# Gathers two steps ahead, each in two halves, and the maxima's three parts summed on VectorE

## The chip, the cores and the metric

The kernel runs on one core of a Trainium2 chip. A core has five engines with queues of their own: TensorE (PE; its weight loads are shown apart, as PEld), VectorE (DVE), ScalarE (ACT), GpSimd (POOL) and SyncE (SP). Each engine works through its own instructions strictly in order, and waits on semaphores for what others make. SP only issues plain DMAs here, and POOL issues the indirect ones (gathers by a list of row numbers). SBUF is the working memory, with 128 partitions; PSUM is what TensorE writes to.

The metric is the device time of one execution in microseconds. Times before: a median of 1243.95 us over 14 runs, from 1241.13 to 1253.4.

## The reference

One layer of attention on a graph of 3125 nodes with 128 features and 100000 edges, of five types. The edges are sorted by destination. For each type r:

```python
q = x[dst] @ W_Q[r]; k = x[src] @ W_K[r]; v = x[src] @ W_V[r]     # 8 heads of 16
logits = (q * k).sum(-1) / 4 + attn_bias[r]
max_v = segment_max(logits, dst)                 # per node, type and head
exp_l = exp(logits - max_v[dst])
attn = exp_l / (segment_sum(exp_l, dst)[dst] + 1e-12)
out += segment_sum(attn * v, dst)
```

Only the edges of type r take part in round r. After that come a projection, a residual and a layer norm, and once more a residual and a layer norm. The result has 3125 x 128 values.

## The kernel before, in words

**Tables.** A first part, up to about 100 us, computes for every pair of node and type the rows of k and v (`kv_d`, 256 values a row), stores them in HBM, and prepares for each edge the number of its row (`idx`). q is computed block by block in the main loop, and stored as three bf16 parts.

**Groups.** The 100000 edges are cut into 196 groups of 512 (`GE`), so that a group is four tiles of 128 edges (`T` = 4). For each group POOL issues four indirect DMAs (`gather`, line 681), one for each tile, each fetching 128 rows of 1 KB into a kv buffer. There are `KVB` = 22 kv buffers, used in turn, each with a pool of its own. Nine of them (`KVA`) lie outside the memory of the first part.

**Steps.** The main loop has steps k from -2 to some 220. Step k does the logits of group k: VectorE multiplies kv with the q of each edge (`prod`, L759), sums over each head (`lg`, L760), and SP stores the result to HBM (L765). The q of each edge comes from TensorE (`qe`, L746), which multiplies a 0/1 matrix `hot` (from `spot`, L737) with the q of the nodes of the group's window. Step k also weighs group v = k - 19, for v from 22 on (16 to 18 behind for the first groups), whose maxima are known by then: `weigh` (L881) multiplies the v half of the kv buffer with the exponentials. It is the last reader of that kv buffer.

**Maxima.** The nodes come in 25 blocks of 128, about eight groups each. One step after the last group that may hold an edge of the block, `maxima_load` issues on POOL one indirect DMA that gathers the stored logits of the block (`ell`, L772, 2304 bytes for each of 128 nodes). In the three steps after that VectorE makes the maxima (`mine` L795, `wl` L810, `mx` L816; before the first of them ScalarE copies `ell` to `by_head`, L787). They are split into three bf16 parts (`m3`), stored, and fetched for each group as `mw` on SP's queue. The block's first group is weighed eight steps after its last logits.

**Spreading the maxima.** One step before a group is weighed, `spread_m` brings the maxima of the nodes to the edges with TensorE: for each of four tiles, and each of the three parts, one matmul (L863) of `hot` with `mw`, the three parts being accumulated in PSUM. Its output is repeated `times` = 8 times (12 where there are no logits to do any more); only the first copy is read. `less_max` (L872, VectorE) subtracts it from the logits, in place in PSUM, `exps` (L876, ScalarE) takes the exponential, and `weigh` and `weights` (L889) read that. `sums` (L915, L917, L924) then sums the weighed rows of each node with TensorE.

**The order.** The order of the instructions on each engine is that in which the loop writes them out. Waits are derived from the buffers: an instruction that writes a buffer waits for the last reader of what was there. In step k the loop writes first SP's fetches, then the gathers of all groups up to k + 2 (`AHEAD` = 2; k + 1 in the last sixteen steps before the last group), then the ell gather if one is due; `spread_m` of the next group, `sums`, `spread_q`; and on VectorE `weigh`, `less_max` (for the next step), `norm` (L936 to L939), `logits`, `spot`, and the step's share of q's remainders (L717, L726), maxima and norms. A step is thus some 2.9 us of VectorE's time in the lightest case, and more with maxima or norms in it.

**Blocks as the prediction uses them.** A block of the loop is taken to be the time from one ell gather's start to the next one's, eight steps apart as a rule.

Of the kernel before, what the change touches and what calls it, by code (L numbers as in the profile page):

```python
# [8 lines left out]
F32 = mybir.dt.float32  # L9
BF16 = mybir.dt.bfloat16  # L10
I32 = mybir.dt.int32
AF = mybir.ActivationFunctionType
ALU = mybir.AluOpType
AX = mybir.AxisListType
# [3 lines left out]
P = 128  # L18
# [4 lines left out]
HEADS = 8  # L23
# [17 lines left out]
T = GE // P  # L41
NGR = -(-E // GE)
# [4 lines left out]
WR = WN * R  # L47
# [6 lines left out]
AHEAD = 2  # L54
# [5 lines left out]
SB = P * E // N // SR  # L60
SPAD = 5
QB = 3
KVB = 22
HELD = 21
KVA = 9


@with_exitstack
# [40 lines left out]
def full_at(n, more=0):  # L109

    last = E // N * n + slack(n) + more
    return -(-min(E, last) // GE) - 1 if n < N else NGR - 1
# [17 lines left out]
NM = len(MB)  # L130


def windowed_path(
# [4 lines left out]
    nc = tc.nc  # L138
# [4 lines left out]
    kv_d = dram.tile([((NT - 1) * P + 64) * R, KVW], F32, name="kv_d")  # L143
# [6 lines left out]
    def keep(name, shape, dt=F32):  # L150
        return const.tile(shape, dt, name=name)

    idx = keep("idx", [P, T, NGR], I32)
# [19 lines left out]
    def buffers(those):  # L173
        for i in those:
            kvs_[i] = ctx.enter_context(tc.tile_pool(name=f"kvp{i}", bufs=1)).tile(
                [P, T, KVW], F32, name=f"kv{i}"
            )

    at_once = range(KVA)
    buffers(at_once)  # L180
# [171 lines left out]
    live = {}  # L352
# [290 lines left out]
    rows, counted = {}, 0  # L643
# [29 lines left out]
    ps = ctx.enter_context(tc.tile_pool(name="ps", bufs=2, space=PSUM))  # L673
    buffers(i for i in range(KVB) if i not in at_once)
    hold = ctx.enter_context(tc.tile_pool(name="hold", bufs=HELD))
    flow = ctx.enter_context(tc.tile_pool(name="flow", bufs=2))
    late_flow = ctx.enter_context(tc.tile_pool(name="late_flow", bufs=2))
    def gather(g):
        kv = kvs_[g % KVB]
        for t in range(T):  # L680
            nc.gpsimd.indirect_dma_start(  # L681
                out=kv[:, t, :], out_offset=None, in_=kv_d[:, :],
                in_offset=bass.IndirectOffsetOnAxis(ap=idx[:, t, g : g + 1], axis=0),
            )


    def fetch_x(name, b):
# [68 lines left out]
    def logits(g):  # L756
        kv, lg = kvs_[g % KVB], live["lg", g]
        prod = flow.tile([P, T, H], F32, name="prod", bufs=1)
        nc.vector.tensor_tensor(prod, kv[:, :, :H], live.pop(("qe", g)), op=ALU.mult)  # L759
        nc.vector.tensor_reduce(  # L760
            lg[:, :, :HEADS], prod.rearrange("p t (k d) -> p t k d", d=HD), AX.X, ALU.add
        )

    def store_logits(g):
        nc.sync.dma_start(  # L765
            lg_d[g * GE : (g + 1) * GE, :].rearrange("(p t) c -> p (t c)", t=T),
            live["lg", g].rearrange("p t c -> p (t c)"),
        )

    def maxima_load(b):  # L770
        ell = late_flow.tile([P, D, LW], F32, name="ell", bufs=1)
        nc.gpsimd.indirect_dma_start(  # L772
            out=ell.rearrange("p s c -> p (s c)"), out_offset=None,
            in_=lg_d[: (full_at(MEND[b], D) + 1) * GE, :],
            in_offset=bass.IndirectOffsetOnAxis(ap=start_i[:, b : b + 1], axis=0),
        )
        live["ell", b] = ell
# [78 lines left out]

    def spread_m(g, times):

        me = ps.tile([P, T, times, 2, HEADS // 2], F32, name="me", tag="me")
        hot, mw = live.pop(("hot", g)), live.pop(("mw", g))  # L860
        for t in range(T):
            for s in range(3):
                nc.tensor.matmul(  # L863
                    me[:, t], hot[:, t, :],
                    mw[:WR, None, :, s, :].to_broadcast([WR, times, 2, HEADS // 2]),
                    start=(s == 0), stop=(s == 2),
                )
        live["mde", g] = me[:, :, 0].rearrange("p t h k -> p t (h k)")

    def less_max(g):  # L870
        mde = live["mde", g]
        nc.vector.tensor_tensor(mde, live.pop(("lg", g))[:, :, :HEADS], mde, op=ALU.subtract)  # L872

# [4 lines left out]
    def weigh(g):  # L878
        wv, kv = late_flow.tile([P, T, PW], F32, name="wv"), kvs_[g % KVB]
        live["wv", g] = wv  # L880
        nc.vector.tensor_tensor(  # L881
            wv[:, :, :H].rearrange("p t (k d) -> p t k d", d=HD),
            kv[:, :, H:].rearrange("p t (k d) -> p t k d", d=HD),
            live["mde", g][:, :, :, None].to_broadcast([P, T, HEADS, HD]),
            op=ALU.mult,
        )
# [131 lines left out]
    step_of, n = {}, 0  # L1018
# [3 lines left out]
    group_at = {k: g for g, k in step_of.items()}  # L1022
    final = step_of[NGR - 1]
# [5 lines left out]
    full_step = [step_of[full_at(n, D)] for n in MEND]  # L1029
# [3 lines left out]
    at_k, k = {}, 0  # L1033
    for v in range(NGR):
        k = max(k + 1, ready[block_of(v, MEND)])
        at_k[v] = k
    v_at = {k: v for v, k in at_k.items()}
# [19 lines left out]

    gathered = 0
    for gathered in range(KVA):
        gather(gathered)  # L1060
    assert all(q_from[b] >= 2 for b in range(QB, NT))
    for k in range(-2, root_at[NT] + 2):
        v, g = v_at.get(k), group_at.get(k)
        q_step = {k - f: b for b, f in enumerate(q_from) if b >= QB and -2 <= k - f <= 5}

        if k >= 0 and k + 3 in group_at:
            fetch_keys(group_at[k + 3])
            fetch_q(group_at[k + 3])
        if -2 in q_step:
            fetch_x("xq", q_step[-2])  # L1070
        for b in range(NT):
            if done_at[b] - 1 == k:
                fetch_x("xr", b)
            if norm_at[b + 1] + 1 == k:
                store_z(b)
        for b in range(NM):
            if ready[b] - 3 == k:
                store_m(b)
        if 5 in q_step:
            store_q(q_step[5])  # L1080
        for u in range(NGR):
            if max(at_k[u] - 3, ready[block_of(u, MEND)] - 2) == k:
                fetch_m(u)

        while gathered < NGR - 1 and step_of[gathered + 1] <= k + (AHEAD if k < final - 16 else 1):
            gathered += 1
            gather(gathered)
        for b in range(NM):
            if full_step[b] + 1 == k:
                maxima_load(b)  # L1090

        for b in range(NT):
            if done_at[b] + 1 == k:
                residual(b)
        if v_at.get(k - 4) is not None:
            by_node(v_at[k - 4])
        if v_at.get(k - 2) is not None:
            carry(v_at[k - 2])
        if 1 in q_step:
            turned(q_step[1])  # L1100
        if 3 in q_step or 4 in q_step:
            second_part()
        if 2 in q_step or 3 in q_step:
            first_part()

        if v_at.get(k + 1) is not None:
            spread_m(v_at[k + 1], 8 if k + 1 in group_at else 12)
        if v_at.get(k - 1) is not None or v_at.get(k - 3) is not None:
            sums(v_at.get(k - 1), v_at.get(k - 3))
        if k + 1 in group_at:  # L1110
            spread_q(group_at[k + 1])

        if v is not None:
            weigh(v)
        if v_at.get(k + 1) is not None:
            less_max(v_at[k + 1])
            exps(v_at[k + 1])
        if v is not None:
            weights(v)
        if k + 1 in group_at:  # L1120
            types(group_at[k + 1])
        if v_at.get(k - 2) is not None:
            norm(v_at[k - 2])
        if g is not None:
            logits(g)
            store_logits(g)
        if k + 2 in group_at:
            spot(group_at[k + 2])
        if v_at.get(k + 1) is not None:
            places(v_at[k + 1], 2 if k >= final - 1 else 0)  # L1130
        if 3 in q_step or 4 in q_step:
            third_part()
        if 2 in q_step or 3 in q_step:
            remainder()
        for b in range(NM):
            whole = MB[b][2] is None
            if ready[b] - 6 == k and whole:
                maxima(b, 0, 2)
            if ready[b] - 5 == k and whole:
                maxima(b, 2, 4)  # L1140
            if ready[b] - 4 == k:
                maxima(b, 4 if whole else 0, R)
        for b in range(NT):
            if done_at[b] == k:
                project(b)
        for b in range(NT + 1):
            if root_at[b] == k:
                roots(b)
            if norm_at[b] == k:
                norms(b)  # L1150
        if 0 in q_step:
            turn_q(q_step[0])
        if 1 in q_step:
            queries(q_step[1], 0, RH)
        if 2 in q_step:
            queries(q_step[2], RH, R)
# [505 lines left out]
```

## Time and profile before

| | |
|---|---|
| median of 14 runs | 1243.95 us |
| the profiled execution, whole | 1242.57 us |
| its span, first to last instruction | 1240.8 us |
| busy: PE, DVE, ACT, POOL | 858.4, 931.2, 633.4, 799.5 us |
| granted TensorE clock, mean | 0.793 |
| gathers of kv | 784, from 89.8 to 1161.2 us |
| ell gathers | 25, from 150.1 to 1169.2 us |
| mean busy time of one gather | 0.95 us |

The page gives for each engine the busy time, its share of the span and the number of instructions. A line of a group of instructions gives the source line, the engine, the operation, the tiles (out<-in), the count, the busy time in us and the mean of one in ns, and after the second bar the idle time of the engine just before them with its main releaser. A line of the waits gives the waiting instruction, what ended the wait, the total in us, the number of waits and the longest. A line of the timeline gives start and duration in us, engine, line, operation and tiles, and in brackets the idle time of the engine before it. The name of a releaser is inferred: it is the last event seen before the wait ended, and not always the cause.

### The profile page before, as it was taken

Reading aid. Unit: us, or ns where it says so; the run is one execution under the profiler, and the core shown is the slowest. Engines: PE = TensorE matmul, PEld = TensorE weight load, DVE = VectorE, ACT = ScalarE, POOL = GpSimd, SP = SyncE. Lnnn points to the kernel's source line nnn. Section 1 sums busy time; section 2 is a strip of 40 time slices with the busy share of each in tenths; the row PEclk is TensorE's granted clock in tenths of the full one; section 3 lists DMA queues with packets and bytes.
Section 4 is the critical chain, followed back from the end, with each engine's and each line's share of the span. In section 5 each row is a group of like instructions: output and inputs, shape, how many; then the busy total and the mean of one; then the engine's idle time right before and its main releaser. Section 6 shows DMA issues by size and latency. Waiting matters only on the chain.

```text
span 1240.8 us, 25686 instructions
## 1 busy us (share of the span) xinstructions
PE 858.4 (69%) x7526; PEld 675.3 (54%) x7526; DVE 931.2 (75%) x2559; ACT 633.4 (51%) x2248; POOL 799.5 (64%) x901
## 2 busy tenths in 40 slices
PE   7984356667676777687777677767767767776784
PEld 3543244456555555566565555555656555565573
DVE  4554376688787778878877887877977878789886
ACT  2560033454564565566456456555645645646463
POOL 1627777776777767676766776766767677767300
PEclk9995556787877878778678788778877878879797
DMA  6997666766676676666676667666666666666300
GB/s 165 322 326 201 169 157 171 184 161 146 180 167 159 170 172 151 168 182 166 155 162 169 159 168 175 149 164 172 163 149 175 161 156 178 169 151 158 93 8 18
DMA packets 180889, 203.63 MB, mean 164 GB/s; under 512 B 83207, under 2 KB 146083, under 8 KB 180620
## 3 DMA queue, kind: packets, MB, share of 16 engines
q0 software_dynamic: 40896, 113.39, 33.2%
q1 hardware_dynamic: 135414, 83.80, 28.9%
q10 hardware_dynamic: 4430, 4.71, 1.5%
q8 instruction: 63, 1.03, 0.3%
q14 instruction: 86, 0.70, 0.2%
HBM read 166.50 MB, written 35.28 MB: 163 GB/s over the span
## 4 chain that ended last, share of the span: by engine, by line
DMA 24%; DVE 24%; PE 21%; issue 12%; POOL 11%; ACT 5%; SPq 2%; DVEq 0%; ACTq 0%; POOLq 0%
POOL kv L681 11%; DMA kv<-kv_d,idx 8%; DMA ell<-lg_d,start_i 6%; PE pp L915 6%; DMA mw<-m_d 4%; DVE wl L810 4%; PE pr L395 4%; DVE prod L759 3%; PE me L863 3%; DVE wv L881 3%; PE qe L746 2%; DVE mx L816 2%; DVE lg L760 2%; PE pp L917 2%; DVE hot L737 2%
## 5 line engine op out<-in xcount | busy, mean ns | idle before, releaser
L681 POOL DMA_INDIRECT kv<-kv_d,idx x784 | 744.8, 950 | 268.1 <-issue 195.9
L915 PE MATMUL pp<-wv,at 128*125 128x136 f32 x1568 | 351.9, 358 | 1.6 <-DVE o L939 1.6
L915 PEld LDWEIGHTS pp<-wv,at 128*125 128x125 f32 x1568 | 264.7, 234 | 62.5 <-issue 60.1
L863 PE MATMUL me<-mw,hot 125*128 125x64 bf16 (+1 forms) x2352 | 127.2, 211 | 162.6 <-DMA mw<-m_d 90.6
L901 ACT ACTIVATE at<-row_at,nkey 128x125 f32<-128x125 f32 x744 | 237.5, 398 | 0.0
L746 PE MATMUL qe<-qw,hot 125*128 125x128 bf16 x2352 | 202.3, 248 | 40.0 <-DVE hot L737 36.6
L863 PEld LDWEIGHTS <-hot 125*128 125x128 bf16 x2352 | 114.1, 110 | 194.3 <-issue 97.4
L876 ACT ACTIVATE me<-me 128x32 f32<-128x32 f32 x196 | 35.7, 182 | 358.9 <-DVE me L872 358.3
L746 PEld LDWEIGHTS <-hot 125*128 125x128 bf16 x2352 | 188.1, 121 | 46.0 <-DVE hot L737 44.1
L759 DVE TENSOR_TENSOR prod<-kv,qe 128x512 f32<-128x512 f32 x196 | 133.0, 678 | 34.7 <-DMA kv<-kv_d,idx 31.5
L760 DVE TENSOR_REDUCE lg<-prod 128x32 f32<-128x512 f32 x196 | 134.5, 686 | 6.8
L881 DVE TENSOR_TENSOR wv<-kv,me 128x512 f32<-128x512 f32 x196 | 132.5, 676 | 4.3 <-PE pp L915 4.2
L917 PE MATMUL pp<-pt,carried 125*5 125x136 f32 x390 | 92.0, 325 | 55.1 <-ACT pt L930 54.2
L904 ACT ACTIVATE at<-at 128x500 f32<-128x500 f32 (+1 forms) x196 | 117.3, 599 | 6.2
L707 PE MATMUL prq<-wq,xTq 128*128 128x384 f32 (+1 forms) x88 | 53.6, 705 | 85.2 <-DVE rem L717 85.2
L872 DVE TENSOR_TENSOR me<-lg,me 128x32 f32<-128x32 f32 x196 | 37.5, 191 | 94.5 <-PE me L863 90.0
L810 DVE TENSOR_TENSOR wl<-by_head,shut 128x1024 f32<-128x1024 f32 (+2 forms) x73 | 76.9, 1053 | 13.7 <-ACT by_head L787 11.0
L816 DVE TENSOR_REDUCE mx<-wl 128x16 f32<-128x1024 f32 (+2 forms) x73 | 76.5, 1048 | 2.5
L924 PEld LDWEIGHTS pp<-rsum,o 125*128 125x128 f32 x392 | 75.9, 236 | 4.2 <-issue 4.1
L737 DVE TENSOR_SCALAR hot<-kt,row_of 125x512 bf16<-125x512 bf16 x196 | 70.9, 362 | 1.5 <-DMA kt<-key_d 1.1
L924 PE MATMUL pp<-rsum,o 125*128 125x25 f32 x392 | 68.8, 258 | 4.0 <-DVE o L939 4.0
L917 PEld LDWEIGHTS pp<-pt,carried 125*5 125x5 f32 x390 | 18.2, 86 | 93.5 <-ACT pt L930 69.9
(184 smaller groups left out, 981.1 us busy)
## 6 DMA issues: line engine op xcount, KB each, us to landing
kt<-key_d SPq DMA_DIRECT2D x196, 128.0 KB
qw<-q_d SPq DMA_DIRECT2D x196, 96.0 KB
kv_d<-kvs SPq DMA_DIRECT2D x24, 640.0 KB
kv<-kv_d,idx POOLq DMA_INDIRECT x784
q_d<-q SPq DMA_DIRECT2D x22, 480.0 KB
lg_d<-lg SPq DMA_DIRECT2D x196, 18.0 KB
mw<-m_d SPq DMA_DIRECT2D x196, 6.0 KB
xr<-in_x SPq DMA_DIRECT2D x24, 64.0 KB
```

What stands on the lines that cost most here:

```text
L681: nc.gpsimd.indirect_dma_start(out=kv[:, t, :], out_offset=None, in_=kv_d[:, :], in_offset=bass.IndirectOffsetOnAxis(ap=idx[:, t, g : g + ...
L746: nc.tensor.matmul(qe[:, t, :], hot[:, t, :], qw[:WR, s, :], start=(s == 0), stop=(s == 2))
L759: nc.vector.tensor_tensor(prod, kv[:, :, :H], live.pop(("qe", g)), op=ALU.mult)
L760: nc.vector.tensor_reduce(lg[:, :, :HEADS], prod.rearrange("p t (k d) -> p t k d", d=HD), AX.X, ALU.add)
L810: nc.vector.tensor_tensor(wl, by_head[:, None].to_broadcast([P, n, nh, D]), shut[:, :n, None, :].to_broadcast([P, n, nh, D]), op=ALU.add,)
L863: nc.tensor.matmul(me[:, t], hot[:, t, :], mw[:WR, None, :, s, :].to_broadcast([WR, times, 2, HEADS // 2]), start=(s == 0), stop=(s == 2),)
L881: nc.vector.tensor_tensor(wv[:, :, :H].rearrange("p t (k d) -> p t k d", d=HD), kv[:, :, H:].rearrange("p t (k d) -> p t k d", d=HD), live ...
L901: nc.scalar.activation(at[:, t, :], row_at[:, :WR], AF.Abs, bias=nkey[:, t, g : g + 1], scale=1.0)
L904: nc.scalar.activation(at[:, on_dve:], at[:, on_dve:], AF.Relu, bias=1.0, scale=-1.0)
L915: nc.tensor.matmul(pp, at[:, t, :], wv[:, t, :], start=(t == 0), stop=(t == T - 1))
L917: nc.tensor.matmul(pp[:R], carried[:WR, g, :], live.pop(("pt", g - 1)), start=False, stop=False,)
L924: nc.tensor.matmul(op, live.pop(("o5", done)), rsum[:WR], start=True, stop=True)
```

## The change

- `gather` takes two of the four tiles of a group at a time. `first_gathers` does t = 0 and 1, with the row numbers out of `idx` as before. `more_gathers` does t = 2 and 3, and takes the row numbers from a small tile `rows`, which VectorE copies from `idx`.
- In step k, the first half for group k + 2 is written out after `weigh`, and the second half, with its copy, after `logits` and its store. The ell gather, if one is due, comes after that. Before, all of this stood ahead of the step's work. The exception for the last steps (k + 1 instead of k + 2) is gone.
- 21 kv buffers instead of 22; six groups instead of nine are gathered ahead of the loop.
- `spread_m` makes one matmul for each tile, four in all, with all three parts side by side, without accumulation, and with five copies (5 x 24 = 120 columns) where it made twelve matmuls with eight copies (64 columns). `less_max` then sums the three parts with a reduction on VectorE into a tile `mde` in SBUF, which takes the place of the one in PSUM. Where twelve copies were made, after the last logits, nothing changes.

```diff
-KVB = 22
+KVB = 21
-KVA = 9
+KVA = 6
...
-    def gather(g):
+    def gather(g, t0, rows):
         kv = kvs_[g % KVB]
-        for t in range(T):
+        for t in range(T // 2):
             nc.gpsimd.indirect_dma_start(
-                out=kv[:, t, :], out_offset=None, in_=kv_d[:, :],
-                in_offset=bass.IndirectOffsetOnAxis(ap=idx[:, t, g : g + 1], axis=0),
-            )
+                out=kv[:, t0 + t, :], out_offset=None, in_=kv_d[:, :],
+                in_offset=bass.IndirectOffsetOnAxis(ap=rows(t), axis=0),
+            )
+
+    def first_gathers(g):
+        gather(g, 0, lambda t: idx[:, t, g : g + 1])
+
+    def more_gathers(g):
+        rows = flow.tile([P, T // 2], I32, name="rows", bufs=3)
+        nc.vector.tensor_copy(rows, idx[:, T // 2 :, g])
+        gather(g, T // 2, lambda t: rows[:, t : t + 1])
...
     def spread_m(g, times):
+        hot, mw = live.pop(("hot", g)), live.pop(("mw", g))
+        if times < 8:
+            me = ps.tile([P, T, times, 2, 3, HEADS // 2], F32, name="me", tag="me")
+            for t in range(T):
+                nc.tensor.matmul(
+                    me[:, t], hot[:, t, :],
+                    mw[:WR, None].to_broadcast([WR, times, 2, 3, HEADS // 2]),
+                    start=True, stop=True,
+                )
+            live["parts", g] = me[:, :, 0].rearrange("p t h s k -> p t h k s")
+            return
...
     def less_max(g):
+        if ("parts", g) in live:
+            mde = flow.tile([P, T, 2, HEADS // 2], F32, name="mde")
+            nc.vector.tensor_reduce(mde, live.pop(("parts", g)), AX.X, ALU.add)
+            live["mde", g] = mde.rearrange("p t h k -> p t (h k)")
         mde = live["mde", g]
         nc.vector.tensor_tensor(mde, live.pop(("lg", g))[:, :, :HEADS], mde, op=ALU.subtract)
...
     for gathered in range(KVA):
-        gather(gathered)
+        first_gathers(gathered)
+        gather(gathered, T // 2, lambda t: idx[:, T // 2 + t, gathered : gathered + 1])
...
-        while gathered < NGR - 1 and step_of[gathered + 1] <= k + (AHEAD if k < final - 16 else 1):
-            gathered += 1
-            gather(gathered)
-        for b in range(NM):
-            if full_step[b] + 1 == k:
-                maxima_load(b)
...
-            spread_m(v_at[k + 1], 8 if k + 1 in group_at else 12)
+            spread_m(v_at[k + 1], 5 if k + 1 in group_at else 12)
...
         if v is not None:
             weigh(v)
+        ahead_of = []
+        while gathered < NGR - 1 and step_of[gathered + 1] <= k + AHEAD:
+            gathered += 1
+            ahead_of.append(gathered)
+            first_gathers(gathered)
...
         if g is not None:
             logits(g)
             store_logits(g)
+        for u in ahead_of:
+            more_gathers(u)
+        for b in range(NM):
+            if full_step[b] + 1 == k:
+                maxima_load(b)
```

More of the change, by code (lines that the diff above doesn't have):

```diff
@@ L857, in spread_m @@
     def spread_m(g, times):
+        hot, mw = live.pop(("hot", g)), live.pop(("mw", g))
[9 more added lines that the diff above has]
+            return
         me = ps.tile([P, T, times, 2, HEADS // 2], F32, name="me", tag="me")
-        hot, mw = live.pop(("hot", g)), live.pop(("mw", g))
         for t in range(T):
```

## The prediction

> **What bounds the kernel now.** I read the page's totals first, then the waits of POOL and DVE, then the timeline of one block. The totals show that no engine is full; POOL's 64% is an understatement, since an indirect gather is counted with 0.95 us and the next one never starts less than 1.25 us after it.
>
> ```profile
> PE 858.4 (69%) x7526; PEld 675.3 (54%) x7526; DVE 931.2 (75%) x2559; ACT 633.4 (51%) x2248; POOL 799.5 (64%) x901
> ...
> L681 POOL DMA_INDIRECT kv<-kv_d,idx x784 | 744.8, 950 | 268.1 <-issue 195.9
> ```
>
> At 1.25 us, 784 gathers and 25 ell gathers are 1011 us of POOL's time. A group costs POOL 5.0 us, a block of eight groups with its ell gather 33 x 1.25 = 41.25 us. Between the ell gathers at 196.46 and 1078.48 lie 20 blocks, 44.1 us each: POOL has under 3 us to spare per block. DVE's waits:
>
> ```profile
> DVE me L872 <- PE me L863: 90.0, 52, 4.5
> DVE mine L795 <- DMA ell<-lg_d,start_i: 56.9, 21, 6.1
> ...
> DVE prod L759 <- DMA kv<-kv_d,idx: 31.5, 14, 5.2
> ```
>
> kv is hardly waited for, and the timeline shows why: gathers run far ahead. Now the block from the ell gather at 634.89 (step 98; the 196 products of L759, counted, number the steps), first POOL:
>
> ```profile
> 634.89 0.94 POOL L772 DMA_INDIRECT ell<-lg_d,start_i  x1 [3.05 <-ACT lg L753]
> 636.13 0.95 POOL L681 DMA_INDIRECT kv<-kv_d,idx  x1 [0.30 <-DVE hot L737]
> ...
> 657.16 0.94 POOL L681 DMA_INDIRECT kv<-kv_d,idx  x1 [1.18 <-DVE den L936]
> ...
> 668.41 1.15 POOL L681 DMA_INDIRECT kv<-kv_d,idx  x1 [0.30 <-issue]
> ...
> 676.12 0.95 POOL L681 DMA_INDIRECT kv<-kv_d,idx  x1 [0.30 <-issue]
> 679.83 0.94 POOL L772 DMA_INDIRECT ell<-lg_d,start_i  x1 [2.77 <-DMA xq<-in_x]
> ```
>
> Then DVE:
>
> ```profile
> 639.54 0.33 DVE L795 SCALAR_TENSOR_TENSOR mine<-slot,deg,ell 128x64 f32<-128x64 f32 x1 [3.58 <-DMA ell<-lg_d,start_i]
> ...
> 644.52 0.68 DVE L881 TENSOR_TENSOR wv<-kv,me 128x512 f32<-128x512 f32 x1
> ...
> 645.86 0.68 DVE L759 TENSOR_TENSOR prod<-kv,qe 128x512 f32<-128x512 f32 x1
> 646.58 0.69 DVE L760 TENSOR_REDUCE lg<-prod 128x32 f32<-128x512 f32 x1
> ...
> 650.16 0.68 DVE L881 TENSOR_TENSOR wv<-kv,me 128x512 f32<-128x512 f32 x1
> ...
> 656.21 0.68 DVE L881 TENSOR_TENSOR wv<-kv,me 128x512 f32<-128x512 f32 x1
> ...
> 668.33 0.42 DVE L726 TENSOR_TENSOR q<-rem,q 128x256 bf16<-128x256 f32 x1
> ```
>
> The reader is to see three things. (1) POOL issues group 101 at 636.13, though its product is due at 651.49; the last gather of a group is issued 7 to 15 us before its product. (2) At 657.16 POOL starts group 105 just after the weighing of step 102 (656.21 to 656.89): with 22 buffers, the gather of group k+3 is released by the weighing of step k, because weighing runs 19 groups behind. (3) The block is a loop: logits stored, ell gathered, a DVE that stands still for 3.58 us, maxima, weighing, buffers free. POOL had finished at 677.07 and waited 2.77 us for the stored logits.
>
> **The change, part by part.** *One buffer less.* With 21 buffers the weighing of step k releases the gather of k+2, not of k+3: every gather that waits starts one step later. *The second half's release.* t = 2 and 3 wait for a copy that DVE makes after the logits of step k. In step 100 the weighing ends at 645.20 and the logits at 647.27; with the added DVE work the copy is done by about 647.7, while POOL, starting at 645.47, needs two gathers, 2.5 us, to 647.97. So this wait adds nothing where the first half waited; where the first half needn't wait it holds POOL to the same instants (the fill at the start). Behind it on POOL stand the next groups and the ell gather, and for ell ACT's by_head and DVE's mine. The copy itself must wait, on DVE, for gathers of three groups earlier: POOL is never that late, nothing.
>
> *POOL's new order in a block,* with E the start of an ell gather. Group 101 follows at once, to E + 6.25. Group 102 needs the weighing of step 100, which needs ell's maxima: that weighing ended at 645.20, E + 10.31; with 0.27 us from release to start (656.89 to 657.16) group 102 starts at E + 10.6. POOL stands still for 4.3 us that it used to fill with groups 102 and part of 103. Group 103 waits for step 101's weighing, 5.64 us later, group 104 for step 102's, 6.05 us after that; both steps are solid DVE work, so DVE's additions (0.36 us a step, below) count twice. From group 104 on, the weighings of steps 103 to 106 are no later than POOL (3.4, 5.4, 4.8, 2.9 us, plus 0.36 each, against 5.0), though step 105's comes within 0.1 us. Groups 104 to 108 take 5 x 5.0 = 25.0 us, and only then the ell gather, which the change leaves behind group 108. Sum: 10.31 + 0.27 + 5.64 + 0.36 + 6.05 + 0.36 + 25.0 = 48.0 us, where this block took 44.94. The wait of 2.77 us for stored logits is gone, swallowed: the logits of step 105 are stored long before. With the means of the 20 blocks (10.11, 5.66, 5.92) it is 47.7.
>
> *Gathers still in time?* Group 105 would be issued from E + 27.8 to 32.8; the last of its four starts at 31.5 and lands some 3.7 us later (the chain shows 3.68 for one), 35.2; its product is due at about 38.5. Nothing.
>
> *VectorE's additions.* The reduction reads 96 elements: L816 takes 0.69 us for 512 and 1.22 for 1024, 1.04 ns each and 0.16 fixed, so 0.26; less_max depends on it, 0.28 with the gap seen between den and its reciprocal. The copy of two elements a row: between 0.06 (the memset of four) and 0.16 (the reciprocal of two), overlapping its neighbours; 0.08. Together 0.36 us, 0.3 to 0.5, times 196 = 70 us of DVE's time, of which two steps a block lie on the path; elsewhere DVE's stand before ell covers it, and it would cost up to five times 0.36 if that were gone.
>
> *TensorE, ScalarE, SP.* Nothing is moved or added on SP and ScalarE; the exponential, 0.18 us, only reads SBUF instead of PSUM. On PE twelve loads and matmuls of 64 columns become four of 120, 768 columns to 480; me's group takes 0.36 to 0.64 us a step, so at most that is saved, and the wait for its PSUM buffer shrinks. I take nothing: where DVE waits for me, POOL is later still. A gain of 0.3 us there offsets the reduction in step 105. If the shorter matmuls let the clock (0.77 in this block) fall, steps 103 to 105 lengthen; bounds -0.3 and +1 us a block.
>
> *The maxima in SBUF.* The weighing now has both inputs in SBUF. The nearest row is L726, two SBUF inputs: at 668.33 it began 0.08 us before a gather, which took 1.15 us instead of 0.95. Of the gathers that began 0.08 to 0.27 us after an L726 did, those whose start it outlasted by 0.15 us did not grow, and those outlasted by 0.22 to 0.45 us grew by 0.09 to 0.33. A weighing of 0.68 us has some 0.54 us in which a gather can begin so, 0.43 of a 1.25 us cycle, and a mean growth of 0.27: 0.12 us a step, 0.5 us over the steps where POOL is the path. Bounds: 0, and 5 x 0.3 = 1.5 us. I take 0.5: 48.2 us a block. The Trainium skill's page "SBUF — State Buffer", section "Who interferes with whom", speaks against this part: a DVE instruction with two SBUF inputs contends with a GpSimd one that reads SBUF, and the second to issue waits out the first. By that rule taken fully a gather beginning anywhere in a weighing would lose 0.34 us on average with chance 0.54, which I estimate at 0.9 us a block, some 10 us more in all.
>
> *The ends.* Six groups up front instead of nine: POOL reaches the second half of group 6 at 122.3, its copy is ready by 118.4; nothing. After the first ell gather (150.05) the copies hold POOL: the second half of group 13 waits for the product of group 11 (159.47), ready at about 161.2, instead of 153.8 when POOL would come; the ell gather of 196.46 moves by some 2.3 us. The last two long intervals, 1078.48 to 1114.84 (36.4 us, seven groups) and to 1156.23 (41.4), were short because the old condition put ell ahead of one group there; they become about 43.3 and 48.2, 6.9 each. From the last ell on the work is as before.
>
> **Sum.** 20 x (48.2 - 44.1) = 82, + 2.3 + 6.9 + 6.9 = 98 us. The profiled execution took 1242.57 us (span 1240.8): 1340.6. The median of the 14 runs is 1.4 above it: 1342.
>
> **Rivals.** *A, the lead was spare:* gathers lead by 7 to 15 us, 3.7 is needed, a step less is harmless; then only DVE's additions show, between nothing (1244) and 0.36 us in six steps of 22 blocks, 47 us (1291). For it: kv is hardly waited for. Against it: the ell gather shares POOL's queue, and its lateness isn't hidden. *B, faster:* the ell gather no longer waits (57 us in all) and PE is lighter; a POOL that never waits takes 41.25 us a block, 20 x 2.85 = 57 us, 1187. It decides if POOL isn't idle between group 101 and step 100's weighing, that is if that weighing came by E + 6.25 instead of 10.3. Ell alone lands 3.7 to 5.9 us after its issue and by_head adds 1.08: against it. *C, worse:* the ell gather, now right behind others, lands later (5.1 us at 1035.88, where POOL did not wait, against about 4.6), the port costs 1.5, and the steps before 105 come out later than POOL by 0.5: 50.2 us a block, 40 us more, 1382.
>
> **How the numbers follow.** Forecast 0.72, C 0.12, A 0.12 (of it 0.03 with no measurable change), B 0.04. The measurement tells 0.3%, 3.7 us, from no change. Faster 0.04, same 0.03, slower 0.93. The range runs from A's upper end to C, 1290 to 1385; the forecast's own, with the bounds of the unknown costs, is 1315 to 1375.
>
> **What would show it.** Right: ell gathers some 48 us apart, with 1.25 us and no wait before each; POOL idle about 4 us once a block, between its first and second group after ell, released by DVE; DVE's wait for ell longer than 3.6 us. Wrong: ell gathers 44 us apart, DVE busy throughout, or DVE waiting for kv in most steps (then the lead was too short, not the queue).

## The result, and the profile after

The changed kernel takes 1358.07 us (median of 13 runs, 1352.65 to 1360.97) against 1247.23 us for the kernel before (62 runs): 1.0885 times as long, 95% interval 1.0864 to 1.0905. The prediction was 1342 us, with a range of 1290 to 1385.

The profiled execution has a span of 1355.1 us, 114.3 more than before. The totals and POOL's two groups of gathers, from the page:

```profile
PE 880.2 (65%) x6110; PEld 679.3 (50%) x6110; DVE 991.6 (73%) x2926; ACT 645.1 (48%) x2248; POOL 814.9 (60%) x901
...
L681 POOL DMA_INDIRECT kv<-kv_d,idx x404 | 392.2, 971 | 268.7 <-DVE mde L892 154.3
L681 POOL DMA_INDIRECT kv<-kv_d,rows x380 | 367.9, 968 | 136.9 <-issue 72.8
```

The reader is to see that VectorE has got 60 us more work, and that nothing is fuller for it: every engine's share has gone down. What is new is the releaser of the gathers. Before, their idle time was "issue"; now 154 us of it end with L892, the reduction that comes on VectorE just after the weighing (the weighing itself is the cause: L892 is only the last event seen). VectorE's waits on data show the other side:

```profile
DVE mine L804 <- DMA ell<-lg_d,start_i: 122.2, 24, 6.2
DVE prod L768 <- DMA kv<-kv_d,rows: 43.6, 29, 4.5
```

VectorE waited for ell 56.9 us before, and 122.2 now. One block on POOL's timeline, from the ell gather at 685.23:

```profile
685.23 0.95 POOL L781 DMA_INDIRECT ell<-lg_d,start_i  x1 [0.30 <-ACT at L927]
686.48 0.94 POOL L681 DMA_INDIRECT kv<-kv_d,idx  x1 [0.30 <-issue]
...
690.23 0.95 POOL L681 DMA_INDIRECT kv<-kv_d,rows  x1 [0.30 <-issue]
696.65 0.95 POOL L681 DMA_INDIRECT kv<-kv_d,idx  x1 [5.47 <-DVE mde L892]
...
702.64 0.95 POOL L681 DMA_INDIRECT kv<-kv_d,idx  x1 [1.29 <-DVE mde L892]
...
708.91 0.96 POOL L681 DMA_INDIRECT kv<-kv_d,idx  x1 [1.57 <-DVE mde L892]
...
729.27 1.27 POOL L681 DMA_INDIRECT kv<-kv_d,idx  x1 [0.30 <-DMA mw<-m_d]
...
734.60 0.95 POOL L781 DMA_INDIRECT ell<-lg_d,start_i  x1 [0.30 <-ACT at L927]
```

And VectorE in the same block:

```profile
690.71 0.33 DVE L804 SCALAR_TENSOR_TENSOR mine<-slot,deg,ell 128x64 f32<-128x64 f32 x1 [5.53 <-DMA ell<-lg_d,start_i]
...
695.69 0.69 DVE L904 TENSOR_TENSOR wv<-kv,mde 128x512 f32<-128x512 f32 x1
696.30 0.25 DVE L892 TENSOR_REDUCE mde<-me 128x32 f32<-128x96 f32 x1
696.58 0.19 DVE L895 TENSOR_TENSOR mde<-lg,mde 128x32 f32<-128x32 f32 x1
...
698.64 0.20 DVE L692 COPY rows<-idx 128x2 int32<-128x2 int32 x1
698.71 0.35 DVE L746 TENSOR_SCALAR hot<-kt,row_of 125x512 bf16<-125x512 bf16 x1
```

POOL makes one group after ell and then stands still for 5.47 us, until the weighing that needs ell's maxima has ended (695.69 + 0.69 = 696.38; the gather starts 0.27 later). The figures in brackets count the 0.30 us that lies between any two gathers. It is held twice more, by 1.29 and 1.57 us, and after that it works without a pause up to the next ell gather, at 734.60, which waits for nothing but its turn. The block takes 49.4 us. VectorE stands still for 5.53 us at ell, because ell itself comes late.

Worked out from the traces, the means over the 20 blocks between the second and the 22nd ell gather, in us from the start of an ell gather to the first gather of each of the groups after it, and to the next ell:

| kernel | ell landed | group 1 | 2 | 3 | 4 | 5 | 8 | next ell |
|---|---|---|---|---|---|---|---|---|
| before | 4.59 | 1.25 | 6.26 | 11.31 | 16.46 | 22.00 | 37.11 | 44.10 |
| after | 5.00 | 1.25 | 10.19 | 16.47 | 22.73 | 28.10 | 43.85 | 48.95 |
| before, last 16 blocks | 4.58 | 1.25 | 6.26 | 11.32 | 16.51 | 22.18 | 37.31 | 44.31 |
| after, last 16 blocks | 5.03 | 1.25 | 10.96 | 16.96 | 23.26 | 28.41 | 44.03 | 49.15 |

"Landed" is the start of `mine`, which reads it. The last two rows leave out the first four of the 20 blocks: in the first three the weighing runs 16 to 18 groups behind for most of the time, and in all four the first weighing comes sooner after ell. The change costs 4.85 us a block, 97 us over 20 blocks, out of 114.3. Up to the first of these ell gathers there are 2.7 us more (199.20 against 196.46), and the two intervals after the last of them cost 7.2 and 7.9 us (43.54 and 49.25 against 36.36 and 41.39). From the last ell gather but one to the end it is 84.1 us, before 84.5.

### The profile page after: what moved, and what is told of

Its sections match the earlier page's. It is cut to its first block, busy times and chain, and to the rows that moved or that the text cites. A ratio compares the mean times of both kernels' runs of the same rounds, so it can differ in the third digit from the quotient of the medians.

```text
span 1355.1 us, 23244 instructions
## 1 busy us (share of the span) xinstructions
PE 880.2 (65%) x6110; PEld 679.3 (50%) x6110; DVE 991.6 (73%) x2926; ACT 645.1 (48%) x2248; POOL 814.9 (60%) x901
## 4 chain that ended last, share of the span: by engine, by line
DVE 40%; DMA 19%; PE 14%; issue 12%; POOL 6%; ACT 6%; SPq 1%; DVEq 1%; ACTq 0%; POOLq 0%
DMA ell<-lg_d,start_i 8%; POOL kv L681 6%; DVE prod L768 6%; DVE wl L819 6%; DVE wv L904 4%; DMA mw<-m_d 4%; DVE lg L769 4%; DVE mx L825 4%; PE pp L938 4%; DMA kv<-kv_d,rows 3%; PE pr L395 3%; DVE mde L892 2%; ACT by_head L796 2%; DVE den L960 2%; DVE mde L895 2%
## 5 line engine op out<-in xcount | busy, mean ns | idle before, releaser
L681 POOL DMA_INDIRECT kv<-kv_d,idx x404 | 392.2, 971 | 268.7 <-DVE mde L892 154.3
L681 POOL DMA_INDIRECT kv<-kv_d,rows x380 | 367.9, 968 | 136.9 <-issue 72.8
L938 PEld LDWEIGHTS pp<-wv,at 128*125 128x125 f32 x1568 | 276.8, 243 | 132.4 <-issue 66.0
L755 PE MATMUL qe<-qw,hot 125*128 125x128 bf16 x2352 | 222.6, 263 | 44.6 <-DVE hot L746 42.7
L755 PEld LDWEIGHTS <-hot 125*128 125x128 bf16 x2352 | 208.3, 129 | 51.4 <-DVE hot L746 48.9
L899 ACT ACTIVATE mde<-mde 128x32 f32<-128x32 f32 x177 | 40.6, 229 | 365.6 <-DVE mde L895 360.3
L872 PE MATMUL me<-mw,hot 125*128 125x120 bf16 x708 | 87.5, 263 | 71.0 <-DMA mw<-m_d 70.9
L904 DVE TENSOR_TENSOR wv<-kv,mde 128x512 f32<-128x512 f32 x177 | 120.2, 679 | 0.3 <-issue 0.2
L872 PEld LDWEIGHTS <-hot 125*128 125x128 bf16 x708 | 63.2, 123 | 101.9 <-DMA mw<-m_d 76.0
L804 DVE SCALAR_TENSOR_TENSOR mine<-slot,deg,ell 128x64 f32<-128x64 f32 x25 | 8.3, 332 | 122.2 <-DMA ell<-lg_d,start_i 122.2
L796 ACT COPY by_head<-ell 128x512 f32<-128x512 f32 x24 | 25.7, 1071 | 138.7 <-DMA ell<-lg_d,start_i 138.7
L892 DVE TENSOR_REDUCE mde<-me 128x32 f32<-128x96 f32 x177 | 44.6, 252 | 56.3 <-PE me L872 34.6
```

The costliest lines, as they stand in the source:

```text
L681: nc.gpsimd.indirect_dma_start(out=kv[:, t0 + t, :], out_offset=None, in_=kv_d[:, :], in_offset=bass.IndirectOffsetOnAxis(ap=rows(t), axis=0),
L755: nc.tensor.matmul(qe[:, t, :], hot[:, t, :], qw[:WR, s, :], start=(s == 0), stop=(s == 2))
L872: nc.tensor.matmul(me[:, t], hot[:, t, :], mw[:WR, None].to_broadcast([WR, times, 2, 3, HEADS // 2]), start=True, stop=True,)
L904: nc.vector.tensor_tensor(wv[:, :, :H].rearrange("p t (k d) -> p t k d", d=HD), kv[:, :, H:].rearrange("p t (k d) -> p t k d", d=HD), live ...
L938: nc.tensor.matmul(pp, at[:, t, :], wv[:, t, :], start=(t == 0), stop=(t == T - 1))
```

## The experiments

The theories. **Q**, that of the prediction: POOL's queue is held two steps ahead, so that it has nothing to do between the first group after ell and the weighing that needs ell, and the next ell gather stands behind the groups that were held up. **V**: VectorE's added work, and the maxima in SBUF, are the cost. **L**: two steps of lead are too short for the transfers themselves. **H**: the copy of the row numbers is what holds POOL, not the buffers.

### The copy, the buffer, and both

The first of these takes the copy away and leaves 21 buffers.

```diff
     def more_gathers(g):
-        rows = flow.tile([P, T // 2], I32, name="rows", bufs=3)
-        nc.vector.tensor_copy(rows, idx[:, T // 2 :, g])
-        gather(g, T // 2, lambda t: rows[:, t : t + 1])
+        gather(g, T // 2, lambda t: idx[:, T // 2 + t, g : g + 1])
```

> The changed kernel, whose second half of a gather takes its row numbers from idx, without the copy; 21 buffers stay. Theory Q (either of the two waits holds POOL to two steps): 1345 to 1360 us, blocks of 48.5 to 49 us, all of POOL's standstill then put down to the weighing. Rival (the copy's wait is needed for the loss): 1265 to 1300 us.

Measured: 1338.9 us, 1.0738 times the kernel before (1.068 to 1.0796), so 19 us less than the change, and below what Q expected (a small miss). Blocks in the steady part are what they were with the copy: from the sixth ell gather to the 22nd it takes 786.8 us, with the copy 786.4. The 19 us lie in the first five blocks: the sixth ell gather starts at 373.43 and with the copy at 391.82. The three blocks from the second ell gather on take 43.3 us on average before, 48.3 in the changed kernel, and 43.3 without the copy. There the weighing runs fewer than 19 groups behind, 21 buffers are enough, and only the copy holds POOL. In the rest either wait is enough, as expected.

The second puts the buffer back and leaves the copy (`KVB = 21` to `KVB = 22`).

> The changed kernel with 22 buffers, the copy kept. Theory Q as the prediction put it: the copy after the logits of step k holds the second half of group k+2 to the same instants as the buffer did, 1345 to 1360 us; POOL's standstill is then split around the next group's first half. If the buffer alone were the cost: 1265 to 1305 us.

Measured: 1358.89 us, 1.0909 (1.0878 to 1.094): all of the loss, with as many buffers as before. POOL's timeline shows the standstill in the place that was expected, in the middle of a group, ahead of its second half:

```profile
690.27 0.95 POOL L781 DMA_INDIRECT ell<-lg_d,start_i  x1 [0.30 <-issue]
691.52 0.95 POOL L681 DMA_INDIRECT kv<-kv_d,idx  x1 [0.30 <-issue]
...
696.54 0.95 POOL L681 DMA_INDIRECT kv<-kv_d,idx  x1 [0.30 <-issue]
697.79 0.95 POOL L681 DMA_INDIRECT kv<-kv_d,idx  x1 [0.30 <-issue]
703.81 0.95 POOL L681 DMA_INDIRECT kv<-kv_d,rows  x1 [5.07 <-DVE hot L746]
```

L746 is the instruction after the copy on VectorE. So H and Q are both right in part: there are two locks on the same door.

The third removes both.

> The changed kernel with 22 buffers and without the copy; the rest of the change stays (the place of the ell gather, the spread with its reduction). Theory Q (POOL's queue, held two steps ahead): this frees POOL to issue two groups after ell instead of one, so its standstill of 5.5 us goes; from ell to the third weighing after it 11.2 + 0.3 + 6.0 + 6.3 = 23.8 us, then four groups of 5.1 us: 44 to 46 us a block, 1265 to 1305 us. Theory V (VectorE's added work and the port are the cost): that work is all still there but for the copy, 1340 to 1358 us.

Measured: 1269.87 us, 1.0202 (1.0176 to 1.0228), with blocks of 44.98 us: 88 of the 111 us are gone. POOL makes two groups after ell and is then held for a moment only:

```profile
643.17 0.95 POOL L779 DMA_INDIRECT ell<-lg_d,start_i  x1 [1.70 <-issue]
...
653.19 0.95 POOL L681 DMA_INDIRECT kv<-kv_d,idx  x1 [0.30 <-issue]
654.70 0.95 POOL L681 DMA_INDIRECT kv<-kv_d,idx  x1 [0.56 <-DVE mde L890]
```

V falls as an account of the whole: VectorE's reduction and the SBUF maxima are all still there.

### Ell ahead of the gathers, everything else as changed

```diff
+        for b in range(NM):
+            if full_step[b] + 1 == k:
+                maxima_load(b)
         ahead_of = []
...
         for u in ahead_of:
             more_gathers(u)
-        for b in range(NM):
-            if full_step[b] + 1 == k:
-                maxima_load(b)
```

> The changed kernel with 21 buffers and the copy as they are, but the ell gather written ahead of the group's first half instead of behind its second half. Theory Q: ell starts 4 to 5 us earlier in the block (held by the stored logits instead of POOL), two groups lie between it and the weighing that needs it, POOL's standstill goes to under 1 us: blocks of 44 to 46.5 us, 1260 to 1310 us. Theory L (the short lead of two steps is the cost, wherever ell stands): 1340 to 1358 us. Theory V: 1340 to 1358 us.

Measured: 1273.97 us, 1.0227 (1.0184 to 1.0271), blocks of 45.62 us. Both locks are closed, the lead is two steps as in the changed kernel, and most of the loss is gone. L falls. POOL's timeline:

```profile
644.81 0.95 POOL L781 DMA_INDIRECT ell<-lg_d,start_i  x1 [3.51 <-DMA mw<-m_d]
646.06 0.95 POOL L681 DMA_INDIRECT kv<-kv_d,idx  x1 [0.31 <-DVE lg L769]
...
654.83 0.95 POOL L681 DMA_INDIRECT kv<-kv_d,rows  x1 [0.30 <-issue]
656.08 0.94 POOL L681 DMA_INDIRECT kv<-kv_d,idx  x1 [0.30 <-issue]
```

POOL now waits ahead of ell for 3.51 us, and then has two groups to make while ell lands, and no standstill. What ell needs is the stored logits; the name after the arrow, a fetch of `mw`, is only the last event seen. The short lead by itself costs little: what is left of the loss, 29.5 us, is 5 us more than the new spread costs alone (next section), and the two intervals overlap. What costs is that the gather which releases the loop stood last in a queue that was itself held by the loop.

### The spread alone, and the gathers alone

The kernel before with the new `spread_m` and `less_max` and 5 copies, and nothing else of the change:

> The kernel before with the new spread alone: four matmuls instead of twelve, the reduction on VectorE, the maxima in SBUF; gathers and buffers as before. Theory Q: the reduction's 0.28 us lies on the path from ell to the next stored logits in up to five steps of a block, less what TensorE gains; POOL has 3 us to spare and takes the port's 0.7: 0 to 1.4 us a block, 1245 to 1280 us. Theory V: nearly all of the 111 us, 1330 to 1358 us.

Measured: 1268.94 us, 1.0191 (1.0165 to 1.0216): 24.5 us of loss, blocks of 45.11 us. The time is the balance of two sides. Over the 20 blocks the reduction adds 156 x 0.28 = 44 us to VectorE's work, and VectorE's idle time falls from 183.5 to 160.2 us; 20 us are left. Its idle time in front of the spread's result alone falls from 84.5 to 54.8 us. How much of the shorter wait comes from TensorE's eight saved loads and matmuls for each group, and how much from VectorE being later, isn't separated.

The changed kernel with the old spread (the hunks on `spread_m`, `less_max` and the number of copies left out):

> The changed kernel with the old spread: twelve matmuls, no reduction, the maxima in PSUM; gathers, copy and 21 buffers as changed. Theory Q: a block loses the two reductions on POOL's path (0.56 us) and the port's growth of the gathers (0.7 us): about 47.7 us, 20 to 30 us less than the whole change, 1325 to 1340 us. Theory V: 1245 to 1275 us. If the two parts' costs didn't overlap, the spread's 24.5 us alone would come off: 1334.

Measured: 1334.87 us, 1.0719 (1.0654 to 1.0784), blocks of 47.97 us. The two parts add up: 89.5 us for the gathers alone against their run of the kernel before (1245.37), 24.5 for the spread alone, 114.0 together; the whole change costs 110.8. The time came out where it was expected, but not by the terms that were named. In the last 16 blocks the second and third weighing after ell follow the one before them after 5.67 and 5.91 us in the kernel before, after 6.00 and 6.30 in the changed kernel, and still after 5.89 and 6.25 here: with two reductions off the path, 0.56 us, only 0.16 came back. On the timeline `hot` (L746), which follows the copy, takes 0.54 us instead of 0.35 in these steps (see the last section). The rest of the 0.91 us by which these blocks are shorter (48.24 against 49.15) is an earlier first weighing (0.19) and less growth and standstill of the gathers (0.56).

The spread alone and the kernel with both locks open come out at the same time (1268.94 and 1269.87), so moving the gathers and halving them shows no cost where POOL isn't held.

### What the maxima in SBUF cost

The reduction writes its sums into a part of the PSUM buffer that nobody reads, instead of a tile in SBUF. The weighing's second input is then in PSUM again.

```diff
             live["parts", g] = me[:, :, 0].rearrange("p t h s k -> p t h k s")
+            live["room", g] = me[:, :, 1, 0].rearrange("p t s k -> p t (s k)")[:, :, :HEADS]
...
-            mde = flow.tile([P, T, 2, HEADS // 2], F32, name="mde")
-            nc.vector.tensor_reduce(mde, live.pop(("parts", g)), AX.X, ALU.add)
-            live["mde", g] = mde.rearrange("p t h k -> p t (h k)")
+            mde = live.pop(("room", g))
+            nc.vector.tensor_reduce(
+                mde.rearrange("p t (h k) -> p t h k", h=2), live.pop(("parts", g)), AX.X, ALU.add
+            )
+            live["mde", g] = mde
```

> The changed kernel, whose reduction writes its sums into an unread part of the same PSUM buffer instead of a tile in SBUF, so that the weighing has one SBUF input again. Theory of the port: the gathers' growth (18.5 us over the run above 0.965 us each, against 3.3 before) falls to 3 to 5 us, and 0.5 to 0.7 us a block goes, 1340 to 1350 us. Rival (the weighing's inputs don't matter; the gathers grow for another reason): the growth stays near 18 us, 1355 to 1362.

Measured: 1348.36 us, 1.0801 (1.074 to 1.0861), about 10 us less than the change, blocks of 48.72 us. The two intervals all but touch (that of the change begins at 1.0864), so the times alone say little more than that there is a gain; the gathers show it clearly. Their growth (the time above 0.945 us, summed over the gathers that took more than 0.965) falls from 18.5 to 7.6 us (3.3 in the kernel before; 3 to 5 was expected), and POOL's page lines from 971 and 968 ns to:

```profile
L681 POOL DMA_INDIRECT kv<-kv_d,idx x404 | 383.0, 948 | 272.6 <-DVE me L893 159.0
L681 POOL DMA_INDIRECT kv<-kv_d,rows x380 | 365.8, 963 | 138.8 <-issue 71.5
```

Sorted by how long after a weighing's start they began, the 33 gathers of the changed kernel that began 0.0 to 0.3 us after it took 1.29 us on average (all but one of them 1.22 or more), those that began 0.5 us after it or later 0.95 to 0.96; with the maxima in PSUM all of these take 0.95. One such pair on the timeline of the changed kernel:

```profile
729.03 0.68 DVE L904 TENSOR_TENSOR wv<-kv,mde 128x512 f32<-128x512 f32 x1
729.27 1.27 POOL L681 DMA_INDIRECT kv<-kv_d,idx  x1 [0.30 <-DMA mw<-m_d]
```

So it is shown that a weighing with both inputs in SBUF delays gathers; what that is worth in time is not. Of the 0.5 to 0.7 us a block that were expected, 0.2 came (48.95 to 48.72), and in the last 16 blocks less than 0.1 (49.15 to 49.08): from group 4 to the next ell the gathers grow by 0.35 us instead of 0.69, but POOL is held for 0.30 instead of 0.20, and ell landed 0.17 us later. 4.1 of the 7.3 us between the two profiled executions lie before the sixth ell gather, and executions of the changed kernel alone differ by 8 us.

### A kernel that is faster than both

If the loop over ell sets the time, it should help to give it a step more. This is the kernel before with the weighing 20 groups behind instead of 19, one kv buffer and one held tile more, and the gathers and ell written after `weigh`:

```diff
-LAG = 8
+LAG = 9
-KVB = 22
-HELD = 21
+KVB = 23
+HELD = 22
...
-        while gathered < NGR - 1 and step_of[gathered + 1] <= k + (AHEAD if k < final - 16 else 1):
-            gathered += 1
-            gather(gathered)
-        for b in range(NM):
-            if full_step[b] + 1 == k:
-                maxima_load(b)
...
         if v is not None:
             weigh(v)
+        while gathered < NGR - 1 and step_of[gathered + 1] <= k + (AHEAD if k < final - 16 else 1):
+            gathered += 1
+            gather(gathered)
+        for b in range(NM):
+            if full_step[b] + 1 == k:
+                maxima_load(b)
```

> The kernel before with weighing one step later (20 groups behind instead of 19), one kv buffer more (23) and one more of the held tiles, the gathers and the ell gather written after the weighing; old spread, no copy. Theory Q: the wait for ell and for the maxima's fetch gets a step of slack, so that VectorE's standstill at ell (2.7 us a block) and part of that for the maxima (4 us) go, while POOL still has its three steps; blocks of 41.5 to 43.5 us, between POOL's 41.3 and now 44.1; 1195 to 1240 us, less 3 us for one more step at the end. Rival (the block is set by VectorE's work and TensorE's clock, not by ell): 1240 to 1255 us.

Measured: 1233.17 us, 0.9898 times the kernel before (0.9866 to 0.993), blocks of 43.31 us. VectorE's wait for ell, 56.9 us before, is all but gone, and other waits have come up in its place, among them one for the projection (`pj`; 5.7 us before). From VectorE's waits in this kernel:

```profile
DVE me L872 <- PE me L863: 57.1, 37, 3.4
DVE prod L759 <- DMA kv<-kv_d,idx: 43.3, 22, 4.8
DVE h L976 <- PE pj L957: 40.2, 20, 2.9
...
DVE mine L795 <- DMA ell<-lg_d,start_i: 4.9, 3, 2.4
```

The gain, 12 us or 1%, is a fifth of what the wait for ell had been; the time lies towards the upper end of what was expected. The 20 blocks are 16 us shorter together, and from the last ell gather but one to the end it takes 6 us more (90.5 against 84.5). The lag, the buffers and the place of the gathers were changed together, so what each brings isn't shown.

### Four runs that are not used

Four kernels had been run before these, on another chip.

> The changed kernel, whose second half of each gather takes its row numbers from idx again, without the copy on VectorE. Theory Q (the queue): POOL's gathers are held by the weighing of the same step, because 21 buffers and a lag of 19 leave two steps; the copy comes due at the same instants, so taking it away changes little: blocks of 48 to 49 us, 1345 to 1360 us. Theory H (the second half's wait on the copy is the cost): 1250 to 1300 us, blocks of 45 us. Theory V (VectorE's added work is the cost): the copy is a fifth of that work, 1335 to 1345.

> The changed kernel with 22 kv buffers again. Theory Q in the form of the prediction: the copy after the logits of step k holds the second half of group k+2 to the same instants as the buffer did, so 1345 to 1360 us, blocks of 48 to 49 us, but POOL's standstill after ell is split: the first half of the next group goes at once, and the second half waits. Rival (the buffer alone is the cost): 1260 to 1300 us, blocks of 45 us.

> The changed kernel with 22 buffers and without the copy: both of what holds POOL to two steps is gone, the rest of the change stays (the order of the ell gather, the spread with its reduction). Theory Q: POOL can issue two groups after ell and doesn't stand still; ell to the group that waits for the third weighing 11.2 + 0.3 + 6.0 + 6.3 = 23.8 us, four groups of 5.1 us after it, 44.2 us a block by POOL, and by the stored logits 44.1 plus up to five times 0.36, so 44 to 46 us; 1265 to 1305 us. Theory V: 1340 to 1358, since VectorE's work is unchanged but for the copy.

> The changed kernel with 21 buffers and the copy, but the ell gather written ahead of the group's first half (after the weighing) instead of behind its second half. Theory Q: the ell gather starts some 4 to 5 us earlier in the block (held by the stored logits instead of by POOL), two groups lie between ell and the weighing that needs it, and POOL's standstill of 5.5 us goes to under 1 us: blocks of 44 to 46.5 us, 1260 to 1310 us. Rival (ell's place in the queue doesn't matter, the lead of two steps does): 1345 to 1358 us, blocks of 49.

On that chip every kernel took 14 to 31% longer than the same kernel elsewhere, the kernel before most of all, 1631.56 us; the four took 1604.28, 1543.67, 1562.1 and 1498.61 us. They say nothing on the theories. The traces show stretches in which PE, DVE and ACT stand still together, for instance for some 3 us each from 706.3 to 709.3 in the last of the four; the profile names no instruction that would hold them (it has "remote" for VectorE and ScalarE, and "issue" for TensorE). Why, and why the order of the kernels turns round there, stays open. The same four kernels are those of `copy_away`, `buffer_back`, `one_step_more` and `ell_before_gathers`.

## Why the prediction was right

**Group 102 waits for the weighing of step 100, POOL stands still for 4.3 us, and ell comes last.** Right, and shown three ways: by the standstill of 5.47 us on the timeline (5.17 beyond the usual 0.30), by freeing POOL (88 us come back) and by moving ell alone (84 us come back).

**The second half's copy holds POOL to the same instants.** Right in the steady part (the copy alone costs all of the loss, and without it a block is no shorter), and right that it acts in the fill. There it does more than the 2.3 us that were put down for one block: the sum charged the next three blocks 4.1 us each as well, like all the others, by the buffer's wait, which does not hold there. The copy stood in for it: with the copy away these blocks take 43.3 us instead of 48.3, and the sixth ell gather comes 18 us sooner. So the number of these blocks came out, but the buffer was not its cause. (The 153.8 given there for group 13 is the row of group 12; group 13's second half started at 158.80 before, which is what 2.3 us follows from. 2.7 were measured.)

**48.2 us a block; 48.95 measured.** Group 104, which waits for the third weighing, was to start at 10.38 + 6.02 + 6.28 = 22.68 on average, and starts at 22.73. That agreement is luck: the first four blocks, where the first weighing comes 9.06 us after ell, start it at 20.61, the last 16, where it comes after 10.69, at 23.26. For these 16 the same sum, with their own means in the kernel before (10.33, 5.67 and 5.91), gives 22.90 for group 104 and 48.4 for the block, and 49.15 was measured. Of the 0.75 us that are missing, 0.36 lies ahead of group 104: ell lands 0.45 us later, and the rest is 0.09 shorter. The other 0.39 is in "groups 104 to 108 take 25.0 us", plus 0.5 for the port: they take 25.89, with 0.69 of growth of the gathers and 0.20 of short standstills. In the run with the old spread the growth there is 0.25, most of it in gathers that begin during `q` (L726 before, L735 here); so the new weighing brings 0.44 of it, as it was sized, and the 0.25 was left out. Whether the block would be shorter by these 0.44 without it, the run with the maxima in PSUM doesn't show. The standstills lie in a stretch where the prediction had the weighings "no later than POOL", one of them within 0.1 us. 0.75 us a block are 15 us, and the prediction was 16 us low.

**VectorE's additions: 0.28 and 0.08 us.** Right as a sum: in the last 16 blocks the two weighings on POOL's path follow the one before them 0.33 and 0.39 us later than before, where 0.36 was forecast for each. On the timeline L892 starts 0.28 us before the subtraction that needs it, and the copy 0.07 us before its successor (its own 0.2 us overlap). They are not independent, as the run without the reduction shows, where the copy alone costs 0.22 and 0.34. VectorE's busy time grew by 60 us, not by 70: the reduction runs for 177 groups, not for 196. Alone, the spread costs 24.5 us, which was not predicted as a run of its own.

**TensorE, ScalarE: nothing.** Right for the block, since the two steps on POOL's path grew by no more than VectorE's additions. VectorE's wait for the spread did fall (84.5 to 50.1 us over the 20 blocks). The twelve matmuls of a group take 0.52 to 0.85 us in the block shown, not 0.36 to 0.64; the four take 0.37 to 0.61. The granted clock fell, from 0.793 to 0.734 on average; in the run of the spread alone it was 0.765, in that of the gathers alone 0.762. ScalarE's exponential took 0.23 us instead of 0.18, which was put at no change.

**Ell lands as before (C was to have it 0.5 us later).** It landed after 5.00 us instead of 4.59: part of rival C was true, and in the mean of all blocks it is hidden. C's reason, that ell stands right behind other gathers, is not shown: with the spread alone, where the order of the gathers is that of the kernel before, it landed after 4.84. Nor does C's row carry it: at 1035.88 `mine` read ell 4.0 us after the gather's start; the 5.1 is the start of ScalarE's copy `by_head`.

**The ends.** 6.9 us each were forecast for the last two long intervals; 7.2 and 7.9 measured.

**The rivals.** A (the lead was spare) is half right in a way that matters: two steps of lead are nearly enough for the transfers, as the run with ell in front shows; they aren't enough for a queue that also holds ell. B (faster) fell by the condition that was given for it: the weighing came 11.2 us after ell in the block shown, not 6.25.

## What to carry to other kernels

A buffer count that is enough for the transfers can still be too small for the queue that issues them: look for the gather (or any instruction) in that queue on which the release of the next buffer depends, and count what stands in front of it. When a queue is lightly loaded on average, ask what it does in the stretch in which the loop's slowest chain runs; work that it may not do then has to be done later, in front of the next turn of that chain. And where two waits hold the same instruction, removing either shows little or nothing (19 us and none here, where both together were worth 88).

## What had not been expected of the hardware

The gathers' delay by a VectorE instruction with two SBUF inputs is sharper than one row had suggested: a gather that begins while the weighing runs is held until about the weighing's end (0.24 us after the weighing's start: 1.27 us instead of 0.95). The Trainium skill's page "SBUF — State Buffer", section "Summary: rules for kernel authors", says that the second of the two to issue waits for the first to finish; the traces agree with that for the gather. For the weighing they show no such wait: the 83 that began during a gather took 0.68 us, like the others.

Other instructions of VectorE are held up when they begin in a part of a gather. `hot` (L746) takes 0.35 us as a rule; in the run with the old spread, the 63 that began 0.5 to 0.6 us after a gather's start took 0.54 on average, and in the changed kernel 12 such took 0.51. Those that began 0.1 to 0.4 us after it, or 0.7 or later, took 0.35. So a shift of 0.1 us between two engines can cost 0.2 us a step.

The last is the chip on which the same kernels ran 14 to 31% longer, with engines standing still together.
